# A root by log and exp, a moved check, and a re-cut last image in a four-layer convolution and attention kernel

## The chip, the cores and the metric

The kernel runs on one core of a Trainium2 chip. Its time is the device time of one execution in microseconds; a median of three executions is given. A profile is one more execution, recorded instruction by instruction. The core's engines work side by side and meet at semaphores: TensorE (PE; its weight loads are PEld), VectorE (DVE), ScalarE (ACT), GpSimd (POOL), and SyncE (SP), which here issues transfers.

## The reference

The input has 16 images of 256 channels and 28 x 28 points. Four layers follow each other:

```python
# layer 0: 3x3 convolution of signs with signs of weights, scaled; norm over the batch; + x
# layer 1: 3x3 convolution, PReLU, gate; 1x1 convolution, PReLU, gate; residuals
# layer 2
out = prelu(binconv(sign(batchnorm(x, g1, b1)), w1), a1)
out = prelu(binconv(sign(batchnorm(out, g2, b2)), w2), a2)
out = batchnorm(out, g3, b3)              # (x - m) * rsqrt(v + 1e-5) * g + b
x = prelu(out + x, a3)
# layer 3: attention over the 784 points of an image, 64 channels inside
q, k, v = Wq @ x, Wk @ x, Wv @ x
attn = softmax(q.T @ k / 8)
x = x + Wp @ (attn @ v)
```

The third norm of layer 2 needs moments over all 16 images, so layer 3 can start only when the last convolution has ended.

## The kernel before, in words

**Layout.** 256 channels are two halves `k` of 128 partitions. An image is cut into two halves of 392 points (`HN`). `P` is 128, `B` 16, `NC_` 7: the number of chunks of 112 keys in attention.

**Layer 2's last convolution** goes block by block over half images (the last half in two quarters). TensorE runs 18 matmuls into one of three PSUM tiles; ScalarE moves it out (L422), VectorE splits the packed values (L424), applies the PReLU (L1272) and takes statistics (L1280). ScalarE also writes squares of values into `doubts` (L1285), signs for the next image (L1236), and SP copies these, moved by one column, into `shifted` (L436), from which the middle taps read.

**The seam.** `norm("l2c", ...)` makes the scale `r` (`sg3`) and the shift (`bg3`): ScalarE takes a root (L147), then loads the table of the exponential (L149) with an activation of scale 0, VectorE inverts the root (L152), makes one Newton step (L141 to L159), and ScalarE makes two columns of shift (L266). `keep_busy` fills TensorE with matmuls that nobody reads.

**Layer 3** is written out by hand: inside `manual_schedule` each engine runs its instructions in the order in which the lines stand. For images 0 and 1, `to_x2` (v * scale + old x, VectorE, L1663), `shifted` (+ shift, ScalarE, L1667) and `prelu` (VectorE, L1671), or `finish_a` (L1468) and `add_x2` (L1675), complete the layer 2 output; for later images the old x is added by a transfer that GpSimd issues (L1470), and `finish_b` (L1477) is the PReLU. Then come, per image: `queries_keys` (L1490, L1500), copies of queries and keys (L1508, L1512), `project_v` and `turn_v` (L1599 to L1609), seven chunks of `scores` with exponentials (L1524, L1528), sums of the exponentials (L1536, L1538: GpSimd takes chunks 0 to 3, VectorE 4 to 6; L1541 joins them), `values` (L1553), `denominators` (L1545), reciprocal, product (L1583, L1587), `project` (L1617) and the add to x (L1628). The steps of neighbouring images are interleaved. `watch` (L1592) keeps the largest denominators.

**The check.** The fast way is right only if some conditions hold. They are collected in `doubts` and `nonzero`, joined by `doubts_so_far` (L1637 to L1641) in the turn of image 3, summed with `worst` at the end (`raise_flag`), and one flag decides whether all is done again in a slower way (it isn't here).

**The last image** has its values in one PSUM tile `av`: chunks 0 and 1 in full width, then (in `leave`) chunks 2 to 6 for the first 196 columns of each half of the image and for the second; then the products (L1815), four projections into PSUM tiles of two pools, four adds and four stores (L1827).

Of the kernel before, what the change touches and what calls it, by code (L numbers as in the profile page):

```python
# [39 lines left out]
P = 128  # L40
B = 16
# [26 lines left out]
STEEP = 1e24  # L68

# [21 lines left out]
def forward(ctx: ExitStack, tc: tile.TileContext, d: dict, out: bass.AP, careful: bool):  # L91
# [38 lines left out]
    doubts = const.tile([P, 4 * NB + 10], F32, name="doubts")  # L130
# [13 lines left out]
    def rsqrt(name, v, half=None, beside=None, then=None):  # L144

        r, t = (const.tile(list(v.shape), F32, name=name + q) for q in ("_r", "_t"))
        A.activation(t, v, AF.Sqrt)  # L147
        if then:
            A.activation(small.tile(list(v.shape), F32, tag="mv", name="table"), v, then, scale=0.0)  # L149
        if beside:  # L150
            beside()
        V.reciprocal(r, t)  # L152
# [87 lines left out]
    def norm(name, moments, gamma, beta, sf=None, then=lambda r: None, late=False, table=None):  # L240
# [15 lines left out]
        r = rsqrt(name, v, half, (lambda: V.tensor_scalar(less, m, -1.0, None, ALU.mult)) if late else None, table)  # L256
# [5 lines left out]
        def shift(b):  # L262
            o = vtile(f"{name}_shift{len(made)}")
            made.append(o)
            for k in range(2):
                A.activation(o[:, k:k + 1], r[:, k:k + 1], AF.Identity, bias=b[:, k:k + 1], scale=less[:, k:k + 1])  # L266
            return o
# [228 lines left out]
    with tc.tile_pool(name="ps_conv", bufs=3, space=PSUM) as psc, \  # L496
# [720 lines left out]
        with tc.tile_pool(name="ph2", bufs=1) as ph:  # L1217
# [37 lines left out]
            def post2(order, alpha, mom, doubt):  # L1255
# [4 lines left out]
                def post(block, ab):  # L1260
# [34 lines left out]
                    squares = [lambda h=h, m=m: square(h, m) for h, _, m in pieces(block) if not careful]  # L1295
                    squares_p = [lambda s=s: square_p(*s) for s in by_sums]
# [23 lines left out]
            if not careful:  # L1320
# [12 lines left out]
                post2(range(B), pv("a2"), mom, doubts[:, 3 * NB:4 * NB]), [], mom, PARTS, shifted=shifted,  # L1333
# [7 lines left out]
            else:  # L1341
                keep_busy(31)
                with tc.manual_schedule(engines={ET.DVE, ET.Activation}):
                    sg3, shift3 = norm("l2c", mom, pv("g3"), pv("b3"), sf2, late=True, table=AF.Exp)
                    bg3 = shift3(b3c)
# [25 lines left out]
    finish = (sg3, bg3, pt, x2d, x2, load_x2, idle)  # L1371
# [52 lines left out]
def attend_unshifted(ctx, tc, d, out, wqk, wv, wp, keys, worst, doubts, flag, pv, finish):  # L1424
# [12 lines left out]
    sg3, bg3, x, x2d, x2, load_x2, idle = finish  # L1437
# [57 lines left out]
    def queries_keys_apart(b, h, qps, kps):  # L1495

        for k in range(2):
            for i, ps in enumerate((qps, kps)):
# [3 lines left out]
                    start=(k == 0), stop=(k == 1),  # L1502
# [7 lines left out]
    def keys_to(b, rows, h, ps, copy=None):  # L1510
        copy = copy or (A.copy if rows else V.tensor_copy)
        copy(  # L1512
            keys[b % 2][64 * rows:64 * rows + 64, :, 2 * h:2 * h + 2, 0:GC].rearrange("p c g i -> p g c i"),
            ps[64:P, h, :HN].rearrange("p (g c i) -> p g c i", g=2, i=GC),
# [15 lines left out]
    def sum_up(b, *cs):  # L1530

        for c in cs:
            late, e = c > 3, es[b, c]
            if c in (1, 5):
                sums[b, late] = buf(f"sum{c}", 2)
                (V if late else nc.gpsimd).tensor_tensor(sums[b, late], es[b, c - 1], e, ALU.add)  # L1536
            elif c in (2, 3, 6):
                (V if late else nc.gpsimd).tensor_tensor(sums[b, late], sums[b, late], e, ALU.add)  # L1538
# [10 lines left out]
    def values(b, c, n=slice(0, HN)):  # L1549
        if c == 0:  # L1550
            avs[b] = one_bank(psav, "av")
        for h in range(2):
            T.matmul(  # L1553
                avs[b][64 * h:64 * h + 64, n], lhsT=va[b % 2][:, c, :], rhs=es[b, c][:, h, n],
                start=(c == 0), stop=(c == NC_ - 1 and n.stop == HN),
            )
# [37 lines left out]
    def project_v(b):  # L1594
        ps = one_bank(pssm, "sm")
        for a in range(2):
            for k in range(2):
                for g in range(4):
# [3 lines left out]
                    )  # L1602
        A.copy(
# [51 lines left out]
    with tc.manual_schedule(engines={ET.PE, ET.Activation, ET.DVE, ET.Pool, ET.SP}):  # L1655
# [21 lines left out]
        for k, n in ((1, one), (0, one), (1, two)):  # L1677
            to_x2(0, k, n)
        for k in (1, 0):
            shifted(0, k, one)  # L1680
            prelu(0, k, one)
        queries_keys(0, 0, ps[0], (1, 0))
# [3 lines left out]
        for k in range(2):  # L1686
            prelu(0, k, two)
        kps = two_banks(pssc, "sc")
        queries_keys_apart(0, 1, ps[1], kps)
# [4 lines left out]
        for rows in range(2):  # L1694
# [315 lines left out]
```

## Time and profile before

| | us |
|---|---|
| runs | 944.53, 944.61, 946.26 |
| median | 944.61 |
| the profiled execution | 944.83 |
| its span, first to last instruction | 943.0 |
| TensorE matmul, busy | 925.4 |
| VectorE, busy | 764.7 |
| ScalarE, busy | 675.4 |
| GpSimd, busy | 158.1 |
| layer 2's last convolution ends | 659.7 |
| first matmul of layer 3 | 667.3 |
| last add | 937.1 |

The granted TensorE clock was 0.999 of full speed. In a line of the profile in order of time stand: start and length in us, engine, line of the kernel, operation, output and inputs, partitions x elements, and how many instructions the row merges; in brackets the idle time of the engine before it, and what ended it. All times in the text count from the first instruction.

### The profile page before, as it was taken

How to read it: one execution, taken by the hardware profiler on the slowest of the kernel's cores; microseconds unless marked ns; L12 is line 12 of the kernel's file. 1: busy time of each engine (PE TensorE's matmuls, PEld its weight loads, DVE VectorE, ACT ScalarE, POOL GpSimd, SP SyncE). 2: the span in 40 equal slices, each digit the busy share in tenths (PEclk: the TensorE clock that was granted, in tenths of full speed). 3: DMA queues.
4: the chain of work that ended last, by engine and by line, in shares of the span. 5: the costliest groups of instructions: out<-in, count | busy, mean ns of one | idle time of the engine just before them, and what ended most of it. 6: DMA issues, size and time to landing. Idle time of an engine off the chain costs nothing.

```text
span 943.0 us, 15081 instructions
## 1 busy us (share of the span) xinstructions
PE 925.4 (98%) x5637; PEld 582.3 (62%) x5642; DVE 764.7 (81%) x1446; ACT 675.4 (72%) x1183; POOL 158.1 (17%) x168
## 2 busy tenths in 40 slices
PE   7999999999999999999999999999999999999996
PEld 3555678788888888887555565556444444444443
DVE  3988798999998899986788887889756768777676
ACT  5765568888888888874777756776777666676653
POOL 3332100000000000000000000000344353443422
PEclk9999999999999999999999999999999999999999
DMA  9887434445533344320566301111052433425213
GB/s 341 280 322 270 161 122 140 164 182 196 200 141 139 143 154 173 144 103 35 209 240 215 114 40 60 79 79 60 5 99 69 97 110 78 129 69 137 69 50 125
DMA packets 40132, 130.68 MB, mean 139 GB/s; under 512 B 4898, under 2 KB 17380, under 8 KB 40052
## 3 DMA queue, kind: packets, MB, share of 16 engines
q1 hardware_dynamic: 33876, 98.71, 29.0%
q0 software_dynamic: 5632, 30.54, 11.7%
q8 instruction: 45, 0.74, 0.3%
q10 hardware_dynamic: 544, 0.40, 0.1%
q14 instruction: 35, 0.29, 0.1%
HBM read 72.67 MB, written 32.11 MB: 111 GB/s over the span
## 4 chain that ended last, share of the span: by engine, by line


## 5 line engine op out<-in xcount | busy, mean ns | idle before, releaser
L814 PE MATMUL cv<-vs,w 128*128 128x392 f32 (+1 forms) x1296 | 272.5, 352 | 0.3 <-DVE vs L141 0.3
L406 PEld LDWEIGHTS <-wpk 128*128 128x128 f16 x1782 | 171.3, 97 | 122.0 <-DVE wpk L331 3.6
L406 PE MATMUL cv<-fpads,wpk 128*128 128x392 f16 (+1 forms) x1338 | 228.3, 325 | 2.3 <-DVE wpk L331 1.3
L814 PEld LDWEIGHTS cv<-vs,w 128*128 128x128 f32 x768 | 143.2, 190 | 6.3
L1528 ACT ACTIVATE es<-sc 128x784 f32<-128x784 f32 x112 | 87.3, 822 | 39.6 <-PE sc L1524 39.4
L814 PEld LDWEIGHTS <-w 128*128 128x128 f16 x768 | 69.4, 99 | 51.9 <-issue 9.3
L1524 PE MATMUL sc<-q,keyswa 64*128 64x392 f32 x448 | 89.7, 513 | 0.9 <-ACT es L1528 0.9
L1553 PE MATMUL av<-es,v 128*64 128x392 f32 (+1 forms) x468 | 81.0, 485 | 0.0
L1272 DVE SCALAR_TENSOR_TENSOR p<-ab,vec 128x392 f32<-128x392 int16 (+1 forms) x132 | 78.0, 604 | 0.0
L422 ACT ACTIVATE ab<-cv 128x392 int16<-128x392 f32 (+1 forms) x66 | 32.1, 486 | 56.0 <-PE cv L406 53.1
L1538 POOL TENSOR_TENSOR sum<-sum,es 128x784 f32<-128x784 f32 x32 | 67.7, 2116 | 2.6 <-ACT es L1528 0.2
L969 POOL DMA_DIRECT2D x2d<-x x16 | 8.6, 535 | 345.2 <-DVE x L963 284.9
L1524 PEld LDWEIGHTS sc<-q,keyswa 64*128 64x128 f32 x448 | 38.8, 186 | 43.9 <-issue 16.0
L406 PE MATMUL cv<-shifted,wpk 128*128 128x392 f16 (+1 forms) x324 | 60.6, 322 | 0.0
L814 PE MATMUL cv<-one_on,w 128*128 128x392 bf16 x240 | 59.5, 329 | 0.0
L1553 PEld LDWEIGHTS av<-es,v 128*64 128x64 f32 x468 | 30.8, 136 | 46.1 <-issue 44.9
L424 DVE SCALAR_TENSOR_TENSOR ab<-ab,cv 128x392 int16<-128x392 int16 (+1 forms) x66 | 36.0, 546 | 27.4 <-ACT ab L422 27.0
L796 ACT CAST vs<-vs 128x840 fp32r<-128x840 bf16 x63 | 54.1, 882 | 2.6 <-DVE vs L141 2.5
L1512 DVE COPY keyswa<-mi 64x392 f32<-64x392 f32 x30 | 15.8, 564 | 49.6 <-ACT q L1508 49.6
L941 PE MATMUL cv<-z,fw 128*128 128x392 f32 x256 | 48.9, 342 | 0.1
L1536 POOL TENSOR_TENSOR sum<-es 128x784 f32<-128x784 f32 x16 | 31.1, 1941 | 101.5 <-ACT es L1528 91.4
L941 PEld LDWEIGHTS cv<-z,fw 128*128 128x128 f32 x256 | 46.1, 188 | 0.9 <-ACT z L933 0.9
(324 smaller groups left out, 1586.3 us busy)
## 6 DMA issues: line engine op xcount, KB each, us to landing
xs<-in_x_dram SPq DMA_DIRECT2D x30, 784.0 KB, 5.0
one_on<-vs SPq DMA_DIRECT2D x60, 209.8 KB, 3.0
x2d<-x POOLq DMA_DIRECT2D x16, 784.0 KB, 3.6
out_dram<-p SPq DMA_DIRECT2D x15, 784.0 KB, 3.6
shifted<-fpads SPq DMA_DIRECT2D x26, 449.8 KB, 2.7
p<-x2d POOLq DMA_DIRECT2D x14, 784.0 KB, 6.7
p<-x2d SPq DMA_DIRECT2D x13, 784.0 KB, 6.4
n0d<-n POOLq DMA_DIRECT2D x16, 392.0 KB, 4.3
```

The source lines that it names most:

```text
L406: T.matmul(pss[j][:, n // size if careful else h, :rows * S].rearrange("p (a b) -> p a b", b=S), lhsT=w[:, n, c, :], rhs=src[:, blocks[j][ ...
L422: A.activation(by_halves(ab[:, 1], blocks[j]), ps, AF.Copy, scale=1.0 / PACK)
L424: V.scalar_tensor_tensor(a, b, -PACK, ps, ALU.mult, ALU.add)
L796: copy(v, w)
L814: T.matmul(ps.rearrange("p (a b) -> p a b", b=S), lhsT=w[:, k, c, u, mo * P:(mo + 1) * P], rhs=one_on[:, u, k, :, 0:S] if moved and c == 1 ...
L941: T.matmul(ps[:, h, :HN], lhsT=w[:, k, mo * P:(mo + 1) * P], rhs=z2[b][:, k, h * HN:(h + 1) * HN], start=(k + i == 0), stop=(k + i == 2),)
L1272: V.scalar_tensor_tensor(p, y, alpha[:, mo:mo + 1], y, ALU.mult, ALU.max, accum_out=mom.sums_at(at, mo)[0] if mom.by_sums(at, mo) else None,)
L1524: T.matmul(ps[:, h, :HN], lhsT=chunk[rows], rhs=qs[b][rows], start=True, stop=True)
L1528: A.activation(e, ps[:, :, :HN], AF.Exp, scale=0.125)
L1536: (V if late else nc.gpsimd).tensor_tensor(sums[b, late], es[b, c - 1], e, ALU.add)
L1538: (V if late else nc.gpsimd).tensor_tensor(sums[b, late], sums[b, late], e, ALU.add)
L1553: T.matmul(avs[b][64 * h:64 * h + 64, n], lhsT=va[b % 2][:, c, :], rhs=es[b, c][:, h, n], start=(c == 0), stop=(c == NC_ - 1 and n.stop == ...
```

## The change

1. **Root by log and exp.** For the third norm, `rsqrt` takes `Ln` and then `Exp` with scale -0.5; the Newton step stays. Two GpSimd operations put the logarithm, divided by 40 and with both signs, into `doubts`, which grows by four columns. The one table load that serves both functions stands in layer 2's last convolution, behind the squares of block (8, 0).
2. **The seam.** The second column of the shift is made first, the other one after the first use. The order of the eight VectorE operations of image 0 changes; keys of its second half are copied in four pieces (two chunks, then five); matmuls of its second half take channel half 1 first. The first sum of exponentials of image 0 goes from GpSimd to VectorE.
3. **Doubts behind image 0.** `doubts_so_far` stands ahead of the loop over images instead of in image 3's turn.
4. **The last image.** Its values go to two PSUM tiles, `av` and half of `spare`, one for each part of the columns; six chunks of the first part run ahead of the denominators. The four projections have four places, in three PSUM tiles, and all are issued ahead of the adds.

```diff
-    def rsqrt(name, v, half=None, beside=None, then=None):
+    def rsqrt(name, v, half=None, beside=None, by_log=False):
         r, t = (const.tile(list(v.shape), F32, name=name + q) for q in ("_r", "_t"))
-        A.activation(t, v, AF.Sqrt)
-        if then:
-            A.activation(small.tile(list(v.shape), F32, tag="mv", name="table"), v, then, scale=0.0)
+        if by_log:
+            log = const.tile(list(v.shape), F32, name=name + "_log")
+            A.activation(log, v, AF.Ln)
+            A.activation(r, log, AF.Exp, scale=-0.5)
+            for i, f in enumerate((1.0, -1.0)):
+                n = 4 * NB + 10 + 2 * i
+                nc.gpsimd.tensor_scalar(doubts[:, n:n + 2], log, f / LOG_SPAN, None, ALU.mult)
+        else:
+            A.activation(t, v, AF.Sqrt)
...
-        V.reciprocal(r, t)
+        if not by_log:
+            V.reciprocal(r, t)
...
+                    if by_log and i == 8 and r0 == 0:
+                        squares.append(lambda: A.preload_act_table_set("natural_log_exp_and_others"))
...
-                    sg3, shift3 = norm("l2c", mom, pv("g3"), pv("b3"), sf2, late=True, table=AF.Exp)
-                    bg3 = shift3(b3c)
+                    sg3, shift3 = norm("l2c", mom, pv("g3"), pv("b3"), sf2, late=True, by_log=True)
+                    bg3 = shift3(b3c, (1,))
...
-        for k, n in ((1, one), (0, one), (1, two)):
-            to_x2(0, k, n)
         for k in (1, 0):
-            shifted(0, k, one)
-            prelu(0, k, one)
-        queries_keys(0, 0, ps[0], (1, 0))
+            to_x2(0, k, one)
+        shifted(0, 1, one)
+        rest_of_shift()
+        shifted(0, 0, one)
+        prelu(0, 1, one)
+        to_x2(0, 1, two)
+        prelu(0, 0, one)
         finish_a(0, two, (0,))
         shifted(0, 1, two)
         add_x2(0, 0, two)
-        for k in range(2):
+        for k in (1, 0):
             prelu(0, k, two)
+        queries_keys(0, 0, ps[0], (1, 0))
         kps = two_banks(pssc, "sc")
-        queries_keys_apart(0, 1, ps[1], kps)
+        queries_keys_apart(0, 1, ps[1], kps, (1, 0))
+        vps = one_bank(pssm, "sm")
+        project_v(0, vps)
...
-        for rows in range(2):
-            keys_to(0, rows, 1, kps, V.tensor_copy)
+        for cs in (slice(0, 2), slice(2, NC_)):
+            for rows in range(2):
+                keys_to(0, rows, 1, kps, V.tensor_copy, cs)
...
-        sum_up(0, 1)
+        sum_up(0, 1, engine=V)
...
         V.transpose(ones.rearrange("p a i -> p (a i)"), turned.rearrange("p a i -> p (a i)"))
+        doubts_so_far()
         for b in range(B - 1):
...
-                if b == 3:
-                    doubts_so_far()
...
-        for c in range(2):
-            values(b, c)
+        parts = [slice(0, HN // 2), slice(HN // 2, HN)]
+        spare = two_banks(psmi, "mi")
+        avs[b] = [t[:, 0:HN // 2] for t in (one_bank(psav, "av"), spare[:, 0, :])]
+
+        def last_values(i, cs):
+            for c in cs:
+                for h in range(2):
+                    T.matmul(
+                        avs[b][i][64 * h:64 * h + 64], lhsT=va[b % 2][:, c, :], rhs=es[b, c][:, h, parts[i]],
+                        start=(c == 0), stop=(c == NC_ - 1),
+                    )
+
+        last_values(0, range(NC_ - 1))
         last = two_banks(pssc, "sc")
...
-            for n in parts:
-                for c in range(2, NC_):
-                    values(b, c, n)
-            up = raise_flag(last[:, 1, :], junk[:, 0:4 * B + 1])
-            for n in parts:
-                V.tensor_tensor(o[:, n], avs[b][:, n], r[:, n], ALU.mult)
+            for i, n in enumerate(parts):
+                last_values(i, range(NC_) if i else range(NC_ - 1, NC_))
+                V.tensor_tensor(o[:, n], avs[b][i], r[:, n], ALU.mult)
+            up = raise_flag(last[:, 1, HN:], junk[:, 0:4 * B + 1])
+            more = two_banks(pssc, "sc")
+            places = (more[:, :, parts[0]], spare[:, :, parts[1]], last[:, :, parts[1]], more[:, :, parts[1]])
+            adds = [project(b, i % 2, ps, parts[i // 2]) for i, ps in enumerate(places)]
             up()
-            adds = [project(b, mo, ps, parts[0]) for mo, ps in enumerate((two_banks(psmi, "mi"), two_banks(pssc, "sc")))]
-            for mo in range(2):
-                adds[mo]()
-                adds.append(project(b, mo, two_banks(psmi, "mi") if mo else two_banks(pssc, "sc"), parts[1]))
-            for mo in range(2, 4):
-                adds[mo]()
+            for add in adds:
+                add()
```

## The prediction

> **What bounds the kernel now.** I read the busy shares first, then the order of time in the four places that the change touches, each time asking which wait ends last there.
>
> ```profile
> PE 925.4 (98%) x5637; PEld 582.3 (62%) x5642; DVE 764.7 (81%) x1446; ACT 675.4 (72%) x1183; POOL 158.1 (17%) x168
> ```
>
> TensorE is all but full: 17.6 us of 943.0 are not matmul. A change that leaves its instructions alone can win only where it stands still or starts late. The change touches the seam into layer 3 (662 to 681 us), image 3 (733 us) and the last image (926 us to the end); one instruction goes into layer 2's last convolution.
>
> The seam, in the order of time:
>
> ```profile
> 663.53 0.20 ACT L147 ACTIVATE l2c_t<-l2c_v 128x2 f32<-128x2 f32 x1 [2.06 <-DVE l2c_v L141]
> 663.75 1.28 ACT L149 ACT_TABLE_LOAD   x1
> ...
> 664.62 1.70 DVE L1663 SCALAR_TENSOR_TENSOR p<-p,l2c_r,x 128x392 f32<-128x392 f32 x3
> ...
> 665.15 0.65 ACT L266 ACTIVATE l2c_shift<-l2c_r,b3c,l2c_less 128x1 f32<-128x1 f32 x2
> ...
> 666.50 1.16 DVE L1671 SCALAR_TENSOR_TENSOR p<-p,vec 128x392 f32<-128x392 f32 x2 [0.17 <-ACT p L1667]
> ...
> 668.21 1.17 DVE L1671 SCALAR_TENSOR_TENSOR p<-p,vec 128x392 f32<-128x392 f32 x2
> ...
> 674.19 3.61 DVE L1671 SCALAR_TENSOR_TENSOR p<-p,vec 128x784 f32<-128x784 f32 x2
> ...
> 674.45 2.52 POOL L1536 TENSOR_TENSOR sum<-es 128x784 f32<-128x784 f32 x1 [11.55 <-ACT es L1528]
> ...
> 676.75 0.93 PE L1490 MATMUL mi<-p,wqk 128*128 128x392 f32 x2
> ...
> 677.86 2.24 PE L1490 MATMUL mi<-p,wqk 128*128 128x392 f32 x6 [0.18 <-DVE p L1671]
> ```
>
> The 1.28 us table load looks like the cost, but from 664.62 to 669.38 VectorE is the one that is full: eight operations with one gap, 0.17 us. And at 674.19 the two PReLUs of image 1 take 3.61 us where such a pair takes 1.97 elsewhere (731.11): the second ran 2.57 us beside POOL's first sum, and TensorE waited for it.
>
> Image 3 (TensorE and VectorE, each in order of time):
>
> ```profile
> 725.86 1.53 PE L1599 MATMUL sm<-p,wv 128*32 128x196 f32 x32
> ...
> 738.12 0.93 PE L1617 MATMUL mi<-o,wp 64*128 64x392 f32 x4 [0.60 <-DVE p L1628]
> ...
> 743.13 1.53 PE L1599 MATMUL sm<-p,wv 128*32 128x196 f32 x32
> ...
> 759.53 1.53 PE L1599 MATMUL sm<-p,wv 128*32 128x196 f32 x32
> ```
> ```profile
> 733.00 0.29 DVE L1637 TENSOR_REDUCE sure<-doubts 128x1 f32<-128x142 f32 x1
> ...
> 733.97 2.61 DVE L1583 RECIPROCAL r<-sm 128x392 f32<-128x392 f32 x1
> ```
>
> L1599 marks one image each: 743.13 - 725.86 = 17.27 us here, 759.53 - 743.13 = 16.40 for the next, and 16.40 or 16.41 for all up to the last. Only this image has the five doubt operations, 0.97 us ahead of the reciprocal.
>
> The end:
>
> ```profile
> 926.35 1.54 PE L1553 MATMUL av<-es,v 128*64 128x392 f32 x8
> ...
> 928.25 0.55 PE L1577 MATMUL sm<-sum,ones 128*64 128x196 f32 x4 [0.36 <-DVE sum L1541]
> ...
> 929.75 3.49 PE L1553 MATMUL av<-es,v 128*64 128x196 f32 x40
> ...
> 933.29 0.63 DVE L1815 TENSOR_TENSOR o<-av,r 128x196 f32<-128x196 f32 x2 [0.87 <-PE av L1553]
> ...
> 935.45 0.60 PE L1617 MATMUL sc<-o,wp 64*128 64x196 f32 x4 [0.81 <-DVE p L1628]
> ...
> 936.58 0.55 DVE L1628 TENSOR_TENSOR p<-mi,p 128x392 f32<-128x392 f32 x1
> ```
>
> Three stands: for the sum, for the whole PSUM tile av though its first half was complete near 931.5, and for a free PSUM place. The last add ends at 937.13; 5.87 us of stores and closing follow.
>
> **The change, part by part.**
>
> *Root by log and exp.* Ln takes the place of Sqrt (0.20), Exp (0.20, from the table row's own 0.20 activation) that of the reciprocal (0.17), with one more hand-over on ScalarE (0.03): VectorE's chain starts 0.04 later, at 664.66. The two doubt operations on POOL read the logarithm while POOL is idle (its next work was at 674.45): nothing. Without the load ScalarE can give shift 1 at 665.03, not 665.53. But VectorE still needs its eight operations (0.54 apart, by the rows). By hand: first halves of to_x2 at 664.66 and 665.20; shift applied to channel half 1 from 665.33 to 665.95; its PReLU 665.98; to_x2 of the second half 666.53; PReLU 667.07; add 667.64; PReLUs 668.13 and 668.68, end 669.30 instead of 669.38. **Gain 0.08**; 1.2 us of ScalarE's gain end in VectorE's queue.
>
> *The table load moves* behind block (8, 0) of the last convolution, before the signs of image 10 (618.83 to 620.80). ScalarE waits 1.38 us before its eviction at 617.92, 0.12 before 620.91, 1.38 before 623.90. The load (1.28) makes signs and one eviction late by 1.2 to 1.3 and is absorbed at the next wait. What is late: the signs end 622.08, and TensorE needs them at 623.70. SP's shifted copy goes out at 622.10 instead of 620.82; its landings took 2.7 (median) to 4.1 us, so it is there at 624.8, and TensorE reads it at 625.69. Three PSUM tiles let a late eviction wait two halves of 2.99. **Cost 0**, with 0.9 us of cover; with a 4.1 us landing 0.5.
> Against this speaks the Trainium skill, "ScalarE: Activation LUTs", section "What ACT_TABLE_LOAD costs": 1283 ns for the load and about 1380 of drain, 2.66 us per switch. By it the copy would land at 626.2, a 0.5 us stall. Here the activation before ended 0.02 us ahead of the load and the next began 0.01 behind it: I take 1.28, and keep 0.5 for the range.
>
> *First sum of image 0 to VectorE, keys in four pieces.* A 64x392 copy takes 0.57; from 128x196 and 128x392 operations (0.36, 0.57) I estimate 0.16 + 1.05 ns a column: 2 x 0.27 + 2 x 0.45 and gaps is 1.55, against 1.17. VectorE's chain for image 1 is 0.3 later, its second PReLU ends near 676.45 instead of 677.80, the sum follows (0.93, by its rows) to 677.3. TensorE then runs all eight query and key matmuls in 2.84 (690.89 to 693.73), where it took 680.03 - 676.75 = 3.28. **Gain 0.44.** What is late next: POOL's two sums start at 677.4 instead of 677.05, take 1.86 each if undisturbed and 2.47 at worst; its load of image 2 then leaves at 681.2 to 681.8 (now 681.39), lands 6.6 later, and image 2's PReLUs end at 689.7 to 690.4. TensorE wants them at 690.4.
>
> *Doubts behind image 0.* Five operations, 0.97, into VectorE's idle 4.06 us before 682.02. Image 3 becomes an ordinary one: 17.27 - 16.41. **Gain 0.86.** If the idle time were gone, it would come back as keys of image 1, which nobody reads before 685.
>
> *Last image.* TensorE first does six chunks of part 0 (12 pairs of 0.166) from 926.35 to 928.4, then denominators at 928.5 (the sum is there at 928.10) to 929.86, one chunk of part 0 and seven of part 1: 16 pairs, end 932.67 instead of 933.24. Narrow pairs stand 0.166 apart and wide ones 0.329, so halving costs nothing. The Trainium skill, "TensorE: Matmul & The Clock Gate", section "Back-to-back issue gap", has 81 ns per matmul at 128 columns and 131 at 512; between them, an estimate, 16 narrow for 8 wide would cost 0.5 more and end TensorE at 933.2. The row is from these very instructions; I take it.
> VectorE's reciprocals stay where they are (929.79, 931.13 to 932.46). The first product starts at 932.4, no longer behind all of av, and ends 932.75; the second (part 1 is in another tile) ends by 933.1. Projection 0 starts at 932.8; 1, 2 and 3 follow without a stand, 0.43 apart at first and then 0.33, and end at 934.4. In the built program the flag waits for projection 2 and the first add for projection 3, since both share tiles with them; so the flag comes at 934.15 (now 933.84) and the adds start at 934.45, not at 933.3. Four adds 0.48 apart: the last ends at 936.45. **Gain 0.68.** The flag's read by the store queues (0.9) is over at 935.1, the first add at 935.0: up to 0.1 for the first store, nothing for the last. The four stores leave 0.48 apart instead of in two pairs; 0.2 MB each, against 446 GB/s in the store of image 14, is 0.45, so they just fit; I keep 0.4 for the range. POOL's drain shifts with the flag to 940.8, ahead of the closing at 942.26 - 0.68.
>
> **Sum**: 0.08 + 0 + 0.44 + 0.86 + 0.68 = 2.06 us. Span 943.0 becomes 940.9, the profiled execution 944.83 becomes 942.8. That one was 0.2 above the median of the runs (944.61), so 942.55, told as **942.5**.
>
> **Rivals.**
> *A, as summed* (0.58): 942.1 to 942.9.
> *B, the end gives its gain back* (0.20): of the four last stores' landings some came 1.1 us after the bulk; bunched stores, or a code fetch that the branch waits for (SP stood 3.1 us behind its branch), keep the closing where it is. Then 1.4: 943.2. For it: the last landing (940.52) is SP's next step but one; against: queues are idle for long by then.
> *C, image 1's gain is lost* (0.13): POOL's load leaves late and TensorE waits at 690.4. Then 1.6: 943.0. For it: no cover at the worst value; against: POOL no longer collides with a PReLU.
> *D, slower* (0.04): the moved load stalls the convolution. It takes 2.66 instead of 1.28 and the copy lands after 4.1: TensorE waits from 625.69 to 627.6, 1.9 us, 944.4; from a landing of 4.3 on it is slower than before. Against: two landings of ten known were over 3.
> *E, more* (0.05): the stores' stragglers vanish too: 941.7.
>
> **How the numbers follow.** About 0.2% (1.9 us) is what a measurement of this kernel can tell from no change. A lies on that line: some three quarters of A and all of E count as faster, some of C too, the rest as the same. Faster 0.55, same 0.41, slower 0.04. The range takes in A, B, C and E: 941.8 to 943.5.
>
> **What would show it.** Right: no table load at 663.7 and one near 618.8; the eight VectorE operations still filling 664.7 to 669.3; image 1's eight query and key matmuls in 2.9; 16.4 between projections of values at image 3; products at 932.4 less the shift of 1.4, four adds in a row. Wrong: a TensorE gap in the convolution near 625.7, one near 690.4, adds that are not in a row, or a closing longer than 5.9 us after the last add.

## The result and the profile after

| | before | after |
|---|---|---|
| median of 22 runs each, us | 944.65 | 943.28 |
| lowest to highest, us | 944.31 to 946.26 | 942.84 to 944.64 |
| the profiled execution, us | 944.83 | 943.39 |
| its span, us | 943.0 | 941.6 |

The ratio after to before is 0.9983, with a 95% interval from 0.9977 to 0.9990: 0.9 to 2.2 us less, 1.6 in the middle, 1.4 by the medians. That is 0.17%, just short of the 0.2% that the prediction took for what a measurement of this kernel can tell from no change; the interval reaches over that line on one side and ends short of 1 on the other. The forecast was 942.5 us; the range to 943.5 holds the time, and it lies where rival B put it, at 943.2.

The parts of the span show why. They are cut at instructions that both kernels have: the end of the last convolution, the first projection of values of an image (L1609 in the kernel after, L1599 before), the last add. The turn of image 3, where the doubts stood, lies between the projections of values of images 4 and 5. The last row, the closing, is taken up below.

| part, us | before | after | difference | forecast |
|---|---|---|---|---|
| start to the end of the convolution | 659.74 | 659.37 | -0.37 | 0 |
| from there to the first projection of values | 10.62 | 10.53 | -0.09 | -0.08 |
| image 0 to image 1 | 9.67 | 9.22 | -0.45 | -0.44 |
| turn of image 3 (image 4 to image 5) | 17.26 | 16.41 | -0.85 | -0.86 |
| last image's projection of values to the end of the last add | 29.96 | 29.20 | -0.76 | -0.68 |
| the closing: last add to the end of the span | 5.91 | 6.96 | +1.05 | 0 |

The first row isn't the change: over 14 profiles of different kernels this part lay between 659.03 and 660.12, and between these two profiles 0.34 of the 0.37 arise in the first 16 us (the 37th matmul of the first convolution starts at 16.13 before and at 15.79 after).

The page of the kernel after, first part (busy time, share of the span, instructions); 17.4 us of 941.6 are not matmul, where it was 17.6 of 943.0:

```profile
PE 924.2 (98%) x5645; PEld 583.1 (62%) x5650; DVE 767.6 (82%) x1448; ACT 675.6 (72%) x1183; POOL 155.2 (16%) x169
```

ScalarE in order of time, kernel after. The load now stands in the convolution, takes its 1.28 us, and the signs follow; at the root two short activations are left:

```profile
618.58 1.28 ACT L1306 ACT_TABLE_LOAD   x1
619.88 1.98 ACT L1245 ACTIVATE fpads<-p,l2b_c,vec 128x784 f16<-128x784 f32 x2
...
663.16 0.20 ACT L150 ACTIVATE l2c_log<-l2c_v 128x2 f32<-128x2 f32 x1 [2.06 <-DVE l2c_v L142]
663.39 0.20 ACT L151 ACTIVATE l2c_r<-l2c_log 128x2 f32<-128x2 f32 x1
```

VectorE in order of time, kernel after: the eight operations of the seam (those not shown follow each other), image 1's PReLUs, which took 3.61 us before, the doubts behind image 0, and image 2's PReLUs:

```profile
664.29 1.16 DVE L1677 SCALAR_TENSOR_TENSOR p<-p,l2c_r,x 128x392 f32<-128x392 f32 x2
665.66 0.63 DVE L1685 SCALAR_TENSOR_TENSOR p<-p,vec 128x392 f32<-128x392 f32 x1 [0.21 <-ACT p L1681]
...
667.76 1.16 DVE L1685 SCALAR_TENSOR_TENSOR p<-p,vec 128x392 f32<-128x392 f32 x2
...
674.10 1.98 DVE L1685 SCALAR_TENSOR_TENSOR p<-p,vec 128x784 f32<-128x784 f32 x2
...
677.04 0.26 DVE L1651 TENSOR_REDUCE sure<-doubts 128x1 f32<-128x146 f32 x1
...
677.60 1.37 DVE L1654 SCALAR_TENSOR_TENSOR sure<-some,sure 128x1 f32<-128x1 f32 x1
...
681.11 1.05 DVE L1524 COPY keyswa<-mi 64x392 f32<-64x392 f32 x2 [1.94 <-ACT q L1520]
...
687.43 1.98 DVE L1489 SCALAR_TENSOR_TENSOR p<-p,vec 128x784 f32<-128x784 f32 x2 [3.32 <-DMA p<-x2d]
```

TensorE in order of time, kernel after:

```profile
625.33 1.16 PE L415 MATMUL cv<-shifted,wpk 128*128 128x392 f16 x6
...
669.90 1.53 PE L1609 MATMUL sm<-p,wv 128*32 128x196 f32 x32
...
676.29 2.90 PE L1502 MATMUL mi<-p,wqk 128*128 128x392 f32 x8
679.12 1.53 PE L1609 MATMUL sm<-p,wv 128*32 128x196 f32 x32
...
689.98 2.90 PE L1502 MATMUL mi<-p,wqk 128*128 128x392 f32 x8
...
724.96 1.53 PE L1609 MATMUL sm<-p,wv 128*32 128x196 f32 x32
...
741.36 1.53 PE L1609 MATMUL sm<-p,wv 128*32 128x196 f32 x32
```

No idle time stands in brackets at 625.33, where the moved load could have shown (the matmuls that read the shifted copy), nor at 689.98, where rival C would have. Image 1's eight query and key matmuls run in one piece of 2.90. 679.12 - 669.90 = 9.22; 741.36 - 724.96 = 16.40.

VectorE and TensorE in order of time at the end, kernel after: products, projections without a stand, flag, four adds in a row, the last ending at 934.64:

```profile
930.59 0.30 DVE L1841 TENSOR_TENSOR o<-av,r 128x196 f32<-128x196 f32 x1
...
930.88 0.36 DVE L1841 TENSOR_TENSOR o<-mi,r 128x196 f32<-128x196 f32 x1
...
931.01 0.60 PE L1631 MATMUL sc<-o,wp 64*128 64x196 f32 x4
931.45 0.50 PE L1631 MATMUL mi<-o,wp 64*128 64x196 f32 x4
931.78 0.83 PE L1631 MATMUL sc<-o,wp 64*128 64x196 f32 x8
932.33 0.15 DVE L1661 TENSOR_SCALAR flag<-sc 1x1 int32<-1x1 f32 x1 [1.09 <-PE sc L1631]
932.66 0.57 DVE L1642 TENSOR_TENSOR p<-sc,p 128x392 f32<-128x392 f32 x1 [0.19 <-PE sc L1631]
933.14 0.56 DVE L1642 TENSOR_TENSOR p<-mi,p 128x392 f32<-128x392 f32 x1
933.61 1.03 DVE L1642 TENSOR_TENSOR p<-sc,p 128x392 f32<-128x392 f32 x2
```

What follows is the stores. The view of the line that issues them: duration of an issue (min, median, max in ns), the first and last start, and the time from issue to landing. First the kernel before:

```profile
L1827 ACTq DMA_DIRECT2D out_dram<-p x2: 379/406/432, 935.0 to 936.7; - x2
L1827 SPq DMA_DIRECT2D out_dram<-p x2: 378/388/397, 935.4 to 937.2; - x2
...
DMA to landing us min/median/max: 2.2/2.4/3.2
```

and the kernel after:

```profile
L1853 ACTq DMA_DIRECT2D out_dram<-p x2: 378/405/432, 933.3 to 934.2; - x2
...
L1853 SPq DMA_DIRECT2D out_dram<-p x2: 398/847/1296, 933.7 to 934.7; - x2
...
DMA to landing us min/median/max: 3.9/4.2/4.2
```

The landing line covers three of the four stores. The landing of the fourth, taken from the end of its last part in the trace, was 3.36 us after its issue before (937.16 to 940.52) and 4.66 after (934.67 to 939.33). So the +1.05 divides thus: last add to last issue 0.03 in both; issue to landing +1.30; landing to the end of the span 2.52 before and 2.27 after, -0.25.

Counted from the last image's projection of values (907.18 before, 905.44 after), the first store is issued no earlier than before: 27.77 us behind it before, 27.81 after, since the flag and the first add now stand behind the projections. Only the second pair is issued earlier, by 0.75 us (29.51 and 29.98 before, 28.76 and 29.23 after). In the trace a store lands in 16 parts; twelve of the last store's had landed after 32.21 us before and after 32.27 in the kernel after. The same bytes begin to leave at the same time (first packets 28.72 and 28.76 us behind it) and are through at the same time, so what the last add wins is waited away behind it.

### The profile page after: what moved, and what is told of

It reads as the page before. It is cut to its first block, busy times and chain, and to the rows that moved or that the text cites. A ratio compares the mean times of both kernels' runs of the same rounds, so it can differ in the third digit from the quotient of the medians.

```text
span 941.6 us, 15103 instructions
## 1 busy us (share of the span) xinstructions
PE 924.2 (98%) x5645; PEld 583.1 (62%) x5650; DVE 767.6 (82%) x1448; ACT 675.6 (72%) x1183; POOL 155.2 (16%) x169
## 4 chain that ended last, share of the span: by engine, by line
PE 90%; DVE 5%; ACT 1%; DMA 1%; issue 1%; SPq 1%; DVEq 0%; ACTq 0%
PE cv L823 29%; PE cv L415 27%; PE sc L1536 9%; PE av L1557 8%; PE cv L950 5%; PE mi L1502 5%; PE sm L1609 2%; PE mi L1631 2%; DVE p L1281 1%; DVE l2c_fin L1289 1%; PE sm L1557 1%; DMA xs<-in_x_dram 1%; PE unused L517 1%; PE gate L918 1%; PE hid L726 1%
## 5 line engine op out<-in xcount | busy, mean ns | idle before, releaser
L1557 PE MATMUL av<-es,v 128*64 128x392 f32 x420 | 76.0, 500 | 0.0
L1557 PEld LDWEIGHTS av<-es,v 128*64 128x64 f32 x420 | 27.4, 136 | 44.7 <-issue 44.6
L1502 PE MATMUL mi<-p,wqk 128*128 128x392 f32 x124 | 45.3, 506 | 0.5 <-DVE p L1685 0.4
```

The source lines that it names most:

```text
L1502: T.matmul(ps[:, h, :HN], lhsT=wqk[:, k, :], rhs=x[b][:, k, h * HN:(h + 1) * HN], start=(k == ks[0]), stop=(k == ks[1]),)
L1557: T.matmul(ps[64 * h:64 * h + 64, :HN], lhsT=w, rhs=e[:, h, :], start=start, stop=stop)
```

## The experiments

Runs of one group were compared with common runs of the kernel before (medians 944.94, 944.80 and 944.62 us). The columns of parts are those of the table above, one profile each.

| run | median us | ratio to before, 95% | seam | image 1 | image 3 | to last add | closing |
|---|---|---|---|---|---|---|---|
| before | 944.65 | 1 | 10.62 | 9.67 | 17.26 | 29.96 | 5.91 |
| after | 943.28 | 0.9983 (0.9977 to 0.9990) | 10.53 | 9.22 | 16.41 | 29.20 | 6.96 |
| e1: last image as before | 943.64 | 0.9988 (0.9979 to 0.9996) | 10.53 | 9.22 | 16.41 | 29.96 | 6.18 |
| e2: last image alone | 944.85 | 0.9998 (0.9989 to 1.0006) | 10.62 | 9.66 | 17.27 | 29.20 | 6.47 |
| e3: two stores for four | 943.25 | 0.9983 (0.9975 to 0.9990) | 10.53 | 9.22 | 16.41 | 29.21 | 6.83 |
| e4: half of the stores | 942.97 | 0.9980 (0.9972 to 0.9989) | 10.53 | 9.22 | 16.41 | 29.21 | 5.84 |
| e5: root alone | 944.42 | 0.9995 (0.9987 to 1.0004) | 10.35 | 9.65 | 17.26 | 29.95 | 6.11 |
| e6: load not moved | 944.56 | 0.9999 (0.9990 to 1.0008) | 11.81 | 9.21 | 16.41 | 29.19 | 6.59 |
| e7: doubts alone | 943.77 | 0.9989 (0.9982 to 0.9996) | 10.62 | 9.64 | 16.41 | 29.95 | 6.02 |
| e8: first sum alone | 944.54 | 0.9995 (0.9986 to 1.0003) | 10.62 | 9.22 | 17.27 | 29.95 | 6.02 |
| e9: other places | 943.26 | 0.9984 (0.9977 to 0.9991) | 10.53 | 9.21 | 16.40 | 28.25 | 7.82 |
| e10: old order of the seam | 943.21 | 0.9984 (0.9976 to 0.9991) | 10.36 | 9.22 | 16.40 | 29.20 | 7.01 |
| e11: store queues swapped | 943.47 | 0.9985 (0.9978 to 0.9991) | 10.53 | 9.21 | 16.40 | 29.20 | 6.89 |
| e12: e9 and e10 together | 942.69 | 0.9974 (0.9964 to 0.9984) | 10.35 | 9.21 | 16.40 | 28.26 | 7.57 |

The parts repeat within 0.03 us, whatever else was changed. The closing doesn't: 5.91 to 6.18 in the five kernels whose stores leave in two pairs (before, e1, e5, e7, e8; mean 6.05), and 6.47 to 7.01 in the six whose four projections are all issued ahead of the adds and whose full output is stored, e9 and e12 aside (after, e2, e3, e6, e10, e11; mean 6.79).

### The last image, taken back and alone

e1, from the kernel after, and e2, from the kernel before, the same edit the other way round:

```diff
-            for i, n in enumerate(parts):
-                last_values(i, range(NC_) if i else range(NC_ - 1, NC_))
-                V.tensor_tensor(o[:, n], avs[b][i], r[:, n], ALU.mult)
...
+            for n in parts:
+                for c in range(2, NC_):
+                    values(b, c, n)
...
-            for add in adds:
-                add()
+            adds = [project(b, mo, ps, parts[0]) for mo, ps in enumerate((two_banks(psmi, "mi"), two_banks(pssc, "sc")))]
+            for mo in range(2):
+                adds[mo]()
+                adds.append(project(b, mo, two_banks(psmi, "mi") if mo else two_banks(pssc, "sc"), parts[1]))
...
```

> The changed kernel with the last image as it was before (values in one PSUM tile, two places in use at a time), all else changed. Theory (the steps' gains add up, the new end wins 0.75 us up to the last add and loses 1.05 behind it): seam, image 1 and image 3 keep their 0.1 + 0.45 + 0.85, the way from the last image's projection of values to the last add is 29.95 us again, the closing behind the last add 5.9, and the time is 0.2 to 0.4 us shorter than the changed kernel's: 1.5 to 1.8 under the kernel before. Rival (the longer closing comes from elsewhere, such as code that is fetched later): the closing stays near 7.0, and the time is 0.7 us longer than the changed kernel's.

> The kernel before with the new last image alone. Theory: 29.2 us to the last add (0.75 less), SP's last store takes some 1.3 us to issue instead of 0.4, the closing takes 7.0, so the time is the same or up to 0.3 us longer than before. Rival (the closing is a property of the whole program): closing 5.9 and 0.7 us shorter than before.

e1 has the last add 0.76 later than the kernel after and a closing 0.78 shorter; e2 has the last add 0.76 earlier than the kernel before and a closing 0.56 longer. e2's time is that of the kernel before, 0.9998. The new last image does its own work in 0.76 us less, and by the profiles nearly all of it is lost in the closing (0.74 between the means of the two groups above). By the times no gain of it can be told from nothing. e1 was expected 0.2 to 0.4 us shorter than the kernel after; by the medians it is 0.4 longer, within the intervals.

### What lengthens the closing

Three causes were open: the fourth issue, which held SP's queue for 1.30 us; the bytes that are on their way at once; the side of the queue that issues last. e3 sends the same bytes in two transfers instead of four:

```diff
-            for n in parts:
-                for mo, queue in enumerate((nc.scalar, nc.sync)):
-                    to, of = (halves(t[:, mo, :])[:, :, n] for t in (out[b], x[b]))
-                    queue.dma_start(out=to, in_=of)
+            for n, queue in zip(parts, (nc.scalar, nc.sync)):
+                to, of = (t.rearrange("p k (h n) -> p k h n", h=2)[:, :, :, n] for t in (out[b], x[b]))
+                queue.dma_start(out=to, in_=of)
```

> The changed kernel with two stores at the end, one for each part of the columns with both halves of the channels, on ScalarE's and SP's queue, in the place of four. Theory (four stores 0.48 us apart hold up the issue of the last one): SP's issue takes 0.4 to 0.8 us, the closing 5.9 to 6.3, the time 0.7 to 1.0 us shorter than the changed kernel's. Rival (the landings' stragglers or the code behind the branch set the closing): it stays at 6.8 to 7.0, and the time is the changed kernel's within 0.2.

e4 leaves out the two stores of the first part of the last image, 0.4 MB of output, and nothing else:

```diff
-            for n in parts:
+            for n in parts[1:]:
```

> The changed kernel without the two stores of the first part of the columns of the last image; those 0.4 MB of the output are left out. Theory: with nothing ahead of it in the queues SP's last store issues in 0.4 us and lands in 2.2 to 3.4, the closing is 5.9 or less, the time 1.0 us shorter than the changed kernel's. Rival: closing 6.8 to 7.0, time the same.

e11 lets ScalarE's queue issue the fourth store:

```diff
-                for mo, queue in enumerate((nc.scalar, nc.sync)):
+                for mo, queue in enumerate((nc.sync, nc.scalar)):
```

> The changed kernel with the queues of the four last stores exchanged: SP first and third, ScalarE second and fourth. Theory (whoever issues the fourth store within 1.5 us waits some 0.9 us): ScalarE's second store takes 1.2 to 1.4 us to issue, SP's two 0.4; the closing stays at 6.4 to 7.0. Rival (it is SP's own stream, with code fetched late): SP's second store takes 1.3, ScalarE's 0.4.

e3's two issues took 0.64 and 0.63 us, so none was held, and the closing stayed at 6.83, the rival's number. In e11 the hold went to ScalarE's queue with the fourth store, as the line of its stores shows, and the closing stayed at 6.89:

```profile
L1853 SPq DMA_DIRECT2D out_dram<-p x2: 378/388/397, 933.5 to 934.3; - x2
L1853 ACTq DMA_DIRECT2D out_dram<-p x2: 437/966/1494, 933.8 to 934.7; - x2
```

The long issue is thus not the cause. With half of the bytes, all else in its place (e4), the stores land about as fast as the second pair of the kernel before (3.2 and 3.4), and the closing is 5.84. The lines of e4's two stores:

```profile
L1853 ACTq DMA_DIRECT2D out_dram<-p x1: 427/427/427, 934.2 to 934.2; - x1
L1853 SPq DMA_DIRECT2D out_dram<-p x1: 398/398/398, 934.7 to 934.7; - x1
...
DMA to landing us min/median/max: 3.0/3.0/3.1
```

e4's time, 0.9980, is only 0.3 us under that of the kernel after, where 1.0 was expected, and inside its interval; the closing's 1.1 us is what the profile says, not the runs.

The transfers' rate in the window 933 to 939.5 us, in 40 slices of 0.16 us (GB/s of all the core's transfers). The kernel after:

```profile
GB/s 0 0 0 0 0 0 0 212 256 301 299 316 285 309 309 280 309 294 193 118 63 140 323 338 323 215 68 58 58 53 39 39 34 115 0 0 0 0 50 0
```

and e4, in the same window:

```profile
GB/s 0 0 0 0 0 0 0 151 50 0 0 0 0 135 318 280 347 340 299 323 285 73 84 39 34 65 0 0 0 0 0 0 50 0 0 50 0 0 0 0
```

The bulk goes at about 300 GB/s, and then a few parts come in at 34 to 84 GB/s: from 937.2 to 938.4 in the kernel after. The 0.4 MB of e4 need 1.3 us of bulk (935.1 to 936.4), the 0.8 MB of the kernel after 2.6, plus a pause near 936.2 behind the held fourth issue. In the kernel before, in the window 935 to 941.5 us, also in 40 slices, the two pairs stand apart:

```profile
GB/s 0 0 0 0 50 77 328 289 367 319 338 328 319 207 0 5 261 280 318 304 369 289 323 159 99 84 39 43 24 19 5 0 0 0 0 50 0 0 0 50
```

The first pair's data (936.0 to 937.3) is through, with no tail, before the second's begins (937.6), and only the second pair's tail sets the end. The pause between them, some 0.4 us, is about all that this stream of 0.8 MB could win by an earlier second pair.

The landings of the single parts tell the bulk from the parts that lag. In the five kernels with two pairs, twelve of the last store's 16 parts had landed 2.26 to 2.28 us behind the last add, and the other four 1.13 to 1.49 later. In five with four stores in a row (after, e2, e6, e10, e11) it was 2.89 to 3.21, and 1.11 to 1.85 later. In the means the bulk is 0.81 longer, the lagging parts add 0.11, and from the last landing to the end of the span it takes 0.19 less. So it is the bulk that lengthens the closing; parts that lag are there in the old end too. In e4 the twelve parts came after 2.32, as in the old end, but the other four only 0.77 later: its short closing isn't owed to the bulk alone.

e9 brings the adds forward: other places for the projections (the first add no longer waits for the fourth projection), and the flag behind the first add:

```diff
-            places = (more[:, :, parts[0]], spare[:, :, parts[1]], last[:, :, parts[1]], more[:, :, parts[1]])
+            places = (more[:, :, parts[0]], last[:, :, parts[1]], spare[:, :, parts[1]], spare[:, :, parts[0]])
             adds = [project(b, i % 2, ps, parts[i // 2]) for i, ps in enumerate(places)]
+            adds[0]()
             up()
-            for add in adds:
+            for add in adds[1:]:
                 add()
```

> The changed kernel with other places for the last projections: the first one alone in its PSUM tile, the second beside the flag, the third and fourth in the tile of the values; the flag is made behind the first add. So the first add waits for projection 0 alone, no longer for all four. Theory (the first add stood 1.05 us for PSUM tiles that it shares with later projections): 28.3 to 28.5 us from the last projection of values to the last add instead of 29.20. The stores are still bunched, now behind the read of the flag, so the closing stays at 6.5 to 7.2, and the time is 0.4 to 0.9 us shorter than the changed kernel's. Rival (the drain of 0.8 MB behind the flag sets the end): the closing grows by what the adds win, time the same within 0.2.

The last add came 0.95 us earlier in its part, and the closing was 0.86 longer, more than the theory's 7.2 at most: the time is that of the kernel after, as the rival had said. A line of its stores, and the rate from 933 to 939.5:

```profile
L1854 SPq DMA_DIRECT2D out_dram<-p x2: 397/425/453, 933.4 to 933.9; - x2
...
DMA to landing us min/median/max: 4.5/4.7/5.2
```
```profile
GB/s 0 0 0 0 0 0 152 381 294 294 290 340 304 314 285 294 275 309 359 294 304 159 128 77 82 72 53 84 24 19 19 19 19 19 70 10 50 0 0 0
```

No issue is held here, the bulk has no pause, and still the last store lands 5.5 us after its issue (933.86 to 939.38). The four land 0.57, 0.65 and 0.62 apart though issued within 0.8 us. The tail sinks to 19 GB/s, a sixteenth of 300: at the end one of the 16 engines seems to be working through its share of the four stores alone. When the data flows sets the end, not when the adds are ready. Twelve of the last store's parts had landed 3.42 us behind the last add and the other four 2.12 later, so in e9 the lagging parts have their share in the loss.

What stays open is why a few parts lag. In the kernel after, 13 of the 16 parts of the first store, which has no store ahead of it, had landed by 935.41, and the other three came at 936.53 to 937.16. In the kernel before all 16 parts of the first store landed within 0.30 us (936.89 to 937.19). So a queue of stores isn't the whole reason.

A fetch of code may be. When TensorE's queue has branched on the flag, 16 KB are fetched on an instruction queue, from 1.15 to 1.2 us behind the branch in the runs where I followed it (before, 936.09 and 937.27; after, 933.10 and 934.25; e9, 933.06 and 934.26). In the kernel after this fetch (1.27 us long) and two of 8 KB (934.61 and 934.82) meet the first stores; in the kernel before it starts when the first pair's data is through. In the five kernels with two pairs, the first pair landed in 2.2 to 2.5 us, and the first store of the second pair, beside or behind the fetch, in 3.2 to 3.7. e4's two, whose data starts when the fetch has 0.4 us left, took 3.0 and 3.1. But no run moved the fetch alone, and the trace doesn't say which DMA engine carried what. The fetch's part is argued, not shown.

### The seam

e5, from the kernel before: the root by log and exp with its load moved, in the old order of the seam and with both columns of shift made at once:

```diff
-                    sg3, shift3 = norm("l2c", mom, pv("g3"), pv("b3"), sf2, late=True, table=AF.Exp)
+                    sg3, shift3 = norm("l2c", mom, pv("g3"), pv("b3"), sf2, late=True, by_log=True)
                     bg3 = shift3(b3c)
... (and the root and its load, as in the diff of the change)
```

> The kernel before with the root by log and exp and the table load moved into the convolution, and nothing else: both columns of the shift ahead of their use, and the seam in the old order. Theory (VectorE is the one that is full at the seam): first projection of values 10.55 to 10.65 us behind the end of the convolution, as before (10.62), time the same within 0.2 us. Rival (the table load was on the path): about 0.5 us earlier, 10.1, and time 0.5 shorter.

e10 is its counterpart from the kernel after: the old order comes back, all else stays:

```diff
-                    bg3 = shift3(b3c, (1,))
+                    bg3 = shift3(b3c)
...
+        for k, n in ((1, one), (0, one), (1, two)):
+            to_x2(0, k, n)
         for k in (1, 0):
-            to_x2(0, k, one)
-        shifted(0, 1, one)
-        rest_of_shift()
-        shifted(0, 0, one)
-        prelu(0, 1, one)
-        to_x2(0, 1, two)
-        prelu(0, 0, one)
+            shifted(0, k, one)
+            prelu(0, k, one)
+        queries_keys(0, 0, ps[0], (1, 0))
...
-        for k in (1, 0):
+        for k in range(2):
             prelu(0, k, two)
-        queries_keys(0, 0, ps[0], (1, 0))
...
-        queries_keys_apart(0, 1, ps[1], kps, (1, 0))
+        queries_keys_apart(0, 1, ps[1], kps, (0, 1))
```

> The changed kernel with the seam's old order: both columns of the shift first, three to_x2, then two PReLUs, and the matmuls of the second half with channel half 0 first; all else as changed. Theory (from the run with the root alone: the new order gives back 0.18 us, since VectorE waits for the first shifted half): 10.35 us from the end of the convolution to the first projection of values instead of 10.53, 9.22 to image 1 as in the changed kernel, VectorE without a gap in its eight operations, time 0.2 us shorter at most. Rival (the order matters only together with the old load): 10.53.

Both measured 10.35 or 10.36: the root alone takes 0.27 from the seam, and the new order gives 0.18 of it back. I had expected next to nothing of e5; the rival's 0.5 was too much. VectorE in order of time in e5:

```profile
664.33 1.70 DVE L1673 SCALAR_TENSOR_TENSOR p<-p,l2c_r,x 128x392 f32<-128x392 f32 x3
665.95 1.16 DVE L1681 SCALAR_TENSOR_TENSOR p<-p,vec 128x392 f32<-128x392 f32 x2
667.03 0.56 DVE L1685 TENSOR_TENSOR p<-p,x 128x392 f32<-128x392 f32 x1
667.62 1.16 DVE L1681 SCALAR_TENSOR_TENSOR p<-p,vec 128x392 f32<-128x392 f32 x2
```

With three operations ahead, ScalarE's two columns and its first shifted half are ready before the first PReLU; VectorE works without a stand and ends 4.45 us after it began (664.33 to 668.78). In the kernel before the same order took 4.76 (664.62 to 669.38): there the table load stood ahead of the columns of shift, and VectorE waited 0.17 at 666.50 for the first shifted half. So the load was on the path, for some 0.3 us. In the kernel after only two operations stand ahead, and VectorE waits 0.21 at 665.66 (the first bracket shown of it); it ends after 4.63 (664.29 to 668.92). By its time e10 can't be told from the kernel after; the 0.17 is the profile's.

e6, from the kernel after, doesn't move the load:

```diff
-                    if by_log and i == 8 and r0 == 0:
-                        squares.append(lambda: A.preload_act_table_set("natural_log_exp_and_others"))
```

> The changed kernel without the instruction that loads the table inside the convolution: the build then puts one load ahead of Ln and another between Ln and Exp. Theory: the first lies in ScalarE's 2 us of waiting for the variance and is hidden, the second (1.28) is on the path of r: VectorE's first operation of layer 3 is 1.3 us later, and the time 1.2 to 1.4 us longer than the changed kernel's. Rivals: both on the path, 2.6 longer; or a load as in the page with 1.38 of drain behind it, 2.7 for the second alone.

ScalarE in order of time in e6 has two loads:

```profile
661.26 1.28 ACT L150 ACT_TABLE_LOAD   x1
663.30 0.20 ACT L150 ACTIVATE l2c_log<-l2c_v 128x2 f32<-128x2 f32 x1 [0.76 <-DVE l2c_v L142]
663.52 1.28 ACT L151 ACT_TABLE_LOAD   x1
664.82 0.20 ACT L151 ACTIVATE l2c_r<-l2c_log 128x2 f32<-128x2 f32 x1
```

The first lies in ScalarE's wait for the variance and costs nothing; the second stands between logarithm and exponential on the path, and the seam is 11.81 - 10.53 = 1.28 longer, the load and no more. The Trainium skill, "ScalarE: Activation LUTs", section "What ACT_TABLE_LOAD costs", has 2.66 us for a switch, of which about 1.38 are a drain; in this trace the logarithm's table gave way to the exponential's without it. Without the moved load the kernel is no faster than before (0.9999).

### The two parts in attention, each alone

e7, from the kernel before:

```diff
         V.transpose(ones.rearrange("p a i -> p (a i)"), turned.rearrange("p a i -> p (a i)"))
+        doubts_so_far()
...
-                if b == 3:
-                    doubts_so_far()
```

> The kernel before with the doubts behind image 0 alone. Theory: image 3 takes 16.41 us from one projection of values to the next instead of 17.26, all others are as before, and the closing of 5.9 stays: time 0.85 us shorter. Rival (the later images wait for something else that absorbs it): image 3 or the next is longer by what was won, time the same.

e8, from the kernel before (`sum_up` gets a parameter for its engine):

```diff
-        sum_up(0, 1)
+        sum_up(0, 1, engine=V)
```

> The kernel before with the first sum of exponentials of image 0 on VectorE alone. Theory (the second PReLU of image 1 was held up by POOL's first sum): that PReLU takes 1.03 us instead of 2.57, the eight query and key matmuls of image 1 take 2.84 instead of 3.28, image 0 to 1 is 9.22 to 9.25 us instead of 9.67, time 0.4 shorter. Rival (the order of the seam did it): 9.67 stays, and the sum on VectorE only fills its idle time.

TensorE in order of time, e7: the turn of image 3 is an ordinary one (742.02 - 725.61 = 16.41).

```profile
725.61 1.53 PE L1599 MATMUL sm<-p,wv 128*32 128x196 f32 x32
...
742.02 1.53 PE L1599 MATMUL sm<-p,wv 128*32 128x196 f32 x32
```

And e8: the query and key matmuls of image 1 in one piece with the old seam (679.15 - 669.93 = 9.22). The second PReLU, 2.57 us beside GpSimd's sum in the kernel before, took 1.03.

```profile
669.93 1.53 PE L1599 MATMUL sm<-p,wv 128*32 128x196 f32 x32
...
676.32 2.90 PE L1490 MATMUL mi<-p,wqk 128*128 128x392 f32 x8
679.15 1.53 PE L1599 MATMUL sm<-p,wv 128*32 128x196 f32 x32
```

Each part is worth what the sum gave it, and needs none of the others. e7's time is below that of the kernel before by more than its interval; e8's 0.4 us is too small for the runs.

### Put together

e12 is e9's and e10's edits in one kernel.

> The changed kernel with both: the other places for the last projections and the seam's old order. Theory: 10.35 at the seam, 28.3 to 28.5 to the last add, time 0.5 to 1.0 us shorter than the changed kernel's, which would be 942.3 to 942.8. Rival: the closing takes back what the adds win, 0.2 shorter.

It measured 942.69 us, 0.9974 of the kernel before (0.9964 to 0.9984), 0.5 us below e9 and e10 beside it, and is the fastest full kernel tried; its theory had 942.3 to 942.8. Over the kernel before the gain is clear; over the kernel after it isn't, since the intervals overlap. By its profile it wins 0.18 at the seam; its last image and closing together take 35.83, against 36.16 in the kernel after and 36.07 in e9.

## Why the prediction was right, and where it wasn't

The range holds the time because rival B, at a chance of 0.20, was in it. The central case A (942.1 to 942.9), the sum, doesn't hold it: the terms up to the last add came within 0.08 us each, and the one behind it didn't.

- *Root by log and exp: 0.08.* Measured 0.09. The times worked out by hand were right for the order as changed, its stand included (to_x2 from 665.20, the PReLU not before 665.98). What the sum didn't see is that the old order, without the load, would have kept 0.27 (e5, e10): of ScalarE's gain a part ends not in VectorE's eight operations but in the stand of 0.21 that the new order puts into them.
- *The table load: cost 0.* Right: no stand at 625.33, neither the 0.5 us of the case against it nor rival D's 1.9. The load took 1.28, the row's number, and the next activation began 0.02 behind it.
- *Image 1: 0.44.* Right at 0.45, by the sum's move alone (e8). Rival C falls: image 2's PReLUs ended at 689.41, ahead of TensorE's 689.98, though VectorE had waited 3.32 us for the load.
- *Doubts behind image 0: 0.86.* Right at 0.85. The five operations took 2.1 us (677.04 to 679.16) instead of 0.97, one of them 1.37; VectorE still idled 1.94 after them, so the cover was enough.
- *Last image: 0.68 to the last add.* 0.76. With everything ahead of it 1.73 us earlier than before (the last image's projection of values began at 905.44, not 907.17), products at 930.59, flag at 932.33 and the first add at 932.66 answer to 932.32, 934.06 and 934.39 in the clock of the kernel before; forecast were 932.4, 934.15 and 934.45. The last value matmul ended at 930.83, or 932.56 in that clock: the rows gave 932.67, and the estimate from the Trainium skill, "TensorE: Matmul & The Clock Gate", section "Back-to-back issue gap", 933.2. The row was the better guide.
- *The failed step: "5.87 us of stores and closing follow", with "nothing for the last" store and "they just fit".* This term of the sum was mis-sized: the closing took 6.96, and one longer than 5.9 was among the prediction's own signs of being wrong. The forecast let 0.2 MB pass in 0.45 us, at 446 GB/s, the highest rate of an earlier store; the four last stores went mostly at 260 to 370 GB/s in the kernel before and at about 300 in the kernel after, 0.67 us a store, more than the 0.48 between the issues. So they didn't fit: 0.8 MB that start no earlier than before (the "up to 0.1 for the first store" was right) aren't through earlier. Rival B named it (bunched stores keep the closing where it is), with 1.4 us for what is left; e1 and e2 show the loss, and the landings that it lies in the bulk. Of the other two things in rival B, the parts that lag are in both ends, and the code fetch is undecided.

The account closes. Of the span's 1.44 us, 0.37 came from ahead of the change, and -0.09 - 0.45 - 0.85 - 0.76 + 1.05 = -1.10 from the change (0.03 is left over, from the other images and rounding). With the mean closings of the two groups (+0.74) the change makes -1.41, or 0.15%; the runs say 0.17%. That is what the seam, image 1 and image 3 are worth: 1.39 us.

## What to carry to other kernels

The last compute instruction isn't the end of a kernel: before forecasting a gain ahead of the last stores, ask whether the first of them leaves earlier too and whether they will still land apart, take their rate from the transfers at that very place, and count the gap between issues against it. Work that ends in a burst of stores may only lengthen the wait for them; here a first pair that left early and alone was worth as much as an earlier last add. A step that takes an engine's operation off a path should be tried without the reordering that comes with it: here the order cost two thirds of what the root had won.

## What the runs showed of the hardware that was not expected

- Four stores of 0.2 MB issued within 1.4 us landed 3.9 to 4.7 us after their issue (the kernel after); the last two of them alone, 3.0 and 3.1 (e4). The slowest parts come in at 19 to 84 GB/s for over 1 us after the bulk of 300 (the kernel after, e9).
- Of four such stores, the issue of the fourth was held: 1.30 us on SP's queue (the kernel after), 1.49 on ScalarE's (e11), 1.16 to 1.35 in e2, e6 and e10. Issued closer together (e9, the last 0.26 behind the third) it took 0.45. The reason isn't known.
- A VectorE operation on 128x1 values took 1.37 us (677.60), where the same one took 0.16 in image 3 of the kernel before. GpSimd adds exponentials beside it (from 677.11, for 3.79); the same operation took 1.09 in e7, beside such additions as well. No run moved the additions away.
